# Edge sums moved to TensorE, and attended values computed one column at a time, in a four-layer stack

## The chip, the cores and the metric

The program runs on one core of a Trainium2 chip, in one launch. The core has TensorE (PE for matmuls, PEld for its weight loads), VectorE (DVE), ScalarE (ACT), GpSimd (POOL) and SyncE (SP), which here issues the DMAs. Everything is float32. SBUF and PSUM have 128 partitions[...]. The metric is device time in microseconds (us), the median over runs.

## What is computed

The input is four images of 56 x 56 positions with 128 channels. Four layers follow each other, each as `x = x + layer(group_norm(x))`. Two of them are touched by the change.

Layer 1, the edge layer, treats each of the 56 rows of an image as 56 nodes and sums over all ordered pairs of nodes in that row:

```python
proj_i = jnp.einsum('blnf,of->blno', x, W1)
proj_j = jnp.einsum('blnf,of->blno', x, W2)
edge = jax.nn.relu(proj_i[:, :, :, None, :] + proj_j[:, :, None, :, :] + be)
edge_sum = edge.sum(axis=3)
node_in = jnp.concatenate([x, edge_sum], axis=-1)
node = jax.nn.relu(jnp.einsum('blnc,oc->blno', node_in, Wn) + bn)
```

Written for one channel and one row, with a(n) from W1 and c(m) from W2 and the bias, the sum over m of relu(a(n) + c(m)) is wanted: 56 x 56 values for each row and channel.

Layer 2 is an attention of 32 heads over time steps, carried out on Fourier coefficients. Of it, only the attended values matter here:

```python
out = jnp.einsum('bhts,bhsd->bhtd', attn_w, vs)
...
projd = _fno_layer(out, wP, wPs, bPs, (H, W))
```

Since the projection adds up the heads, what is needed for each of 32 spectral columns c and 56 spectral rows r is the sum over heads h and steps s of attention(h, t, s) times a complex number d(h, c, r) times the complex spectrum x(s, c, r).

Layer 0 (window and global attention, MLP) and layer 3 (a convolution over rows and sums) are the same before and after.

## The kernel before

`build` runs layers 0 and 1 image by image (`first_layers`: window attention, global attention, MLP, then `edge_layer`, L539) and stores each image in `x2d`. Then it computes layer 2's spectra of all images (`spectra`), the weights d (`value_weights`), the attention weights (`attention_weights`), the attended values (`attend`, L916, and `attended_rows`, L973), and last, image by image, `operator_block` and `conv_layer`. Tiles come from pools; a pool's `bufs` is the number of copies that rotate, and a writer waits until the readers of the copy that it takes over are done. Except in the global attention of layer 0, whose TensorE order is written out by hand, the framework orders each engine's instructions, and adds the waits.

**Edge layer.** Channels lie on the partitions. A block (28 in all, 7 for each image) is 8 rows of 56 nodes, 448 columns. TensorE makes a (`e_pi`, L554) and c (`e_pj`, L558) in PSUM; ScalarE copies both into SBUF (`e_a`, L556; `e_c`, L560). For each of the 8 rows, a tile `e_e` of 56 x 56 = 3136 values per partition is filled with a(n) + c(m), on VectorE for even rows (L567, which reads c from PSUM) and on GpSimd for odd rows (L565, both operands from SBUF). ScalarE applies relu in place (L568), and VectorE sums over m (L569, `tensor_reduce` into `e_sum`). There are 4 copies of `e_e`. Two accumulated matmuls with Wn (L571, L572), relu with bias on ScalarE (`e_o`, L574) and an addition on VectorE (L575) end the block.

**Attended values.** `value_weights` writes d in three real combinations to DRAM (`dd`). `attend` runs over 4 groups of 8 columns, 3 combinations and 2 pairs of images. It loads d, spread over 56 partitions, into `u_d` (L932); ScalarE copies the spectrum into PSUM (`u_px`, L944). VectorE (L953, x from PSUM) multiplies into `u_ud`, GpSimd (L955, x from SBUF) into `u_up`, and TensorE (L958) sums over heads and steps with the attention `AT` as the stationary operand and 448 columns moving. `attended_rows` then transposes the result `y` on TensorE into `yh`, partitions by (re/im, r).

**Attention weights**, which the change leaves alone but which the prediction reads: for each head and for both q and k, VectorE multiplies (`q_a`, L863) and multiplies and adds (L867), GpSimd multiplies (`q_c`, L865) and adds (`q_q`, L869), VectorE adds a bias (L870), all on SBUF operands of 1792 (L870: 112) values per partition.

Of the kernel before, what the change touches and what calls it, by code (L numbers as in the profile page):

```python
# [39 lines left out]
def blk(j):  # L40
    return slice(j * NB, (j + 1) * NB)
# [496 lines left out]

def edge_layer(k, w, x1):  # L539

    nc, tc = k.nc, k.tc
    xf = x1.rearrange("p l n -> p (l n)")
    with ExitStack() as es:
# [6 lines left out]
        es_ = big.tile([P, HH, HH], F32, name="e_sum")  # L550
        esf = es_.rearrange("p l n -> p (l n)")
        for j in range(NBLK):
            pi = psum.tile([P, 512], F32, tag="pi", name="e_pi")
            nc.tensor.matmul(pi[:, :NB], w.W1, xg[:, blk(j)], start=True, stop=True)  # L554
            a = wk.tile([P, 8, HH], F32, name="e_a")
            nc.scalar.activation(a.rearrange("p l n -> p (l n)"), pi[:, :NB], AF.Identity, bias=w.be)  # L556
            pj = psum.tile([P, 512], F32, tag="pj", name="e_pj")
            nc.tensor.matmul(pj[:, :NB], w.W2, xg[:, blk(j)], start=True, stop=True)  # L558
            c = wk.tile([P, 8, HH], F32, name="e_c")
            nc.scalar.copy(c.rearrange("p l n -> p (l n)"), pj[:, :NB])  # L560
            pj3 = pj[:, :NB].rearrange("p (l n) -> p l n", l=8)
            for l in range(8):
                e = wk.tile([P, HH, HH], F32, name="e_e", bufs=4)
                if l % 2:
                    nc.gpsimd.tensor_add(e, bc(a[:, l, :], 2, HH), bc(c[:, l, :], 1, HH))  # L565
                else:
                    nc.vector.tensor_add(e, bc(a[:, l, :], 2, HH), bc(pj3[:, l, :], 1, HH))  # L567
                nc.scalar.activation(e, e, AF.Relu)  # L568
                nc.vector.tensor_reduce(es_[:, 8 * j + l, :], e, AX.X, ALU.add)  # L569
            po = psum.tile([P, 512], F32, tag="mm", name="e_po")  # L570
            nc.tensor.matmul(po[:, :NB], w.Wn[:, 0, :], xg[:, blk(j)], start=True, stop=False)  # L571
            nc.tensor.matmul(po[:, :NB], w.Wn[:, 1, :], esf[:, blk(j)], start=False, stop=True)  # L572
            o = wk.tile([P, NB], F32, name="e_o")
            nc.scalar.activation(o, po[:, :NB], AF.Relu, bias=w.bn)  # L574
            nc.vector.tensor_add(xf[:, blk(j)], xf[:, blk(j)], o)  # L575


def l1_host(i):
    We, Wn = i["L1_conv_We"], i["L1_conv_Wn"]
    return {  # L580
        "w1_W1": We[:, :P].T, "w1_W2": We[:, P:].T, "w1_be": i["L1_conv_be"].reshape(P, 1),
        "w1_Wn": Wn.T.reshape(2, P, P).transpose(1, 0, 2), "w1_bn": i["L1_conv_bn"].reshape(P, 1),
    }
# [176 lines left out]
def spectra(k, w, st, x2d):  # L760

    nc, tc = k.nc, k.tc
    with ExitStack() as es:
# [3 lines left out]
        for b in range(B):  # L767
# [23 lines left out]
            for c0 in range(0, 32, 4):  # L791
                ps = psum.tile([P, 512], F32, tag="acc", name="s_px")
                for i in range(4):
                    for ri in range(2):
                        nc.tensor.matmul(ps[:112, i * 112:(i + 1) * 112], z[:, ri, c0 + i, :], k.fv[:, 0, ri, :],
                                         start=(ri == 0), stop=(ri == 1))
                copy(k, c0 // 4, st.xh[:, b, :, c0:c0 + 4, :].rearrange("p i c r -> p c i r"),
                     ps[:112, :448].rearrange("p (c i r) -> p c i r", c=4, i=2))


def value_weights(k, I, w, dd):
# [3 lines left out]
    with ExitStack() as es:  # L805
# [18 lines left out]
        f = wk.tile([P, 3, 8, HH], F32, name="d_f")  # L824
# [4 lines left out]
        nc.scalar.copy(f[:, 0], d[:, 0])  # L829
        nc.vector.tensor_sub(f[:, 1], d[:, 1], d[:, 0])  # L830
        nc.vector.tensor_add(f[:, 2], d[:, 0], d[:, 1])
        nc.sync.dma_start(dd.rearrange("n g h i x -> (g h i) n x"), f.rearrange("p n c r -> p n (c r)"))


def attention_weights(k, I, w, st):

    nc, tc = k.nc, k.tc
    with ExitStack() as es:
# [63 lines left out]
        for bp in range(2):  # L902
# [4 lines left out]
            for h0 in range(0, 16, 4):  # L907
                pt = psum.tile([P, 4, P], F32, tag="mm", name="q_pt")
                for i in range(4):
# [3 lines left out]
                     pt[:112].rearrange("p h (b t) -> p h b t", b=2))  # L913


def attend(k, st, dd):  # L916

    nc, tc = k.nc, k.tc  # L920
    with ExitStack() as es:
        dk = es.enter_context(tc.tile_pool(name="u_dk", bufs=3))
        wk = es.enter_context(tc.tile_pool(name="u_wk", bufs=2))
        psum = es.enter_context(tc.tile_pool(name="u_ps", bufs=2, space=PSUM))
        for g in range(4):
            cs = slice(8 * g, 8 * g + 8)
            for n in (1, 2, 0):
                d = []
                for i in range(2):
                    t = dk.tile([112, 8, NB], F32, tag="d", name="u_d")  # L930
                    for h2 in range(2):
                        nc.sync.dma_start(t[56 * h2:56 * h2 + 56].rearrange("p h x -> p (h x)"),  # L932
                                          dd[n, g, h2, 8 * i:8 * i + 8].rearrange("h x -> (h x)").partition_broadcast(HH))
                    d.append(t)
                for bp in range(2):
                    bs = slice(2 * bp, 2 * bp + 2)
                    if n:
                        x = st.xh[:, bs, n - 1, cs, :].rearrange("p b c r -> p b (c r)")
                    else:
                        x = wk.tile([112, 2, NB], F32, name="u_x")  # L940
                        nc.gpsimd.tensor_add(x, *(st.xh[:, bs, i, cs, :].rearrange("p b c r -> p b (c r)")
                                                  for i in range(2)))
                    px = psum.tile([112, 2, 512], F32, name="u_px")
                    nc.scalar.copy(px[:, :, :NB], x)  # L944
                    po = psum.tile([P, 512], F32, tag="acc", name="u_po")
                    left = 16

                    for i in (0, 1) if bp == 0 else (1, 0):
                        for h0, m, e in ((0, 2, "d"), (5, 2, "p"), (2, 2, "d"), (4, 1, "d"), (7, 1, "p")):
# [235 lines left out]
```

## Time and profile before

| what | us |
|---|---|
| median of 3 runs (7187.75 to 7190.51) | 7190.48 |
| time of the profiled execution | 7190.51 |
| its span, from the first to the last instruction | 7188.7 |
| edge layer of the first image, `e_xg` to the last `e_o` (766.0 to 1072.0) | 306 |
| the same of the other three images (from 1813.9, 2861.8, 3913.1) | 306 each |
| `attention_weights` (4533.7 to 5294.9) | 761 |
| `attend`, first `u` to the last (5295.1 to 5645.2) | 350 |
| `attended_rows` (5645.3 to 5661.6) | 16 |

Times in views of the profile count from the first instruction. A row of the groups reads: line, engine, operation, output and inputs with shapes, number of instructions, then busy us in total, mean ns of one, and the idle time of the engine just before them with what ended it. A row of the timeline reads: start us, length us, engine, line, operation, tiles, how many instructions it merges, and in brackets the idle time before it and what ended that. One float32 matmul of the program shows as two MATMUL records, each with its own weight load. A duration counts from the moment that the engine takes up an instruction; a wait for a memory port lies within it.

### The profile page before, as it was taken

Reading aid. Unit: us, or ns where it says so; the run is one execution under the profiler, and the core shown is the slowest. Engines: PE = TensorE matmul, PEld = TensorE weight load, DVE = VectorE, ACT = ScalarE, POOL = GpSimd, SP = SyncE. Lnnn points to the kernel's source line nnn. Section 1 sums busy time; section 2 is a strip of 40 time slices with the busy share of each in tenths; the row PEclk is TensorE's granted clock in tenths of the full one; section 3 lists DMA queues with packets and bytes.
Section 4 is the critical chain, followed back from the end, with each engine's and each line's share of the span. In section 5 each row is a group of like instructions: output and inputs, shape, how many; then the busy total and the mean of one; then the engine's idle time right before and its main releaser. Section 6 shows DMA issues by size and latency. Waiting matters only on the chain.

```text
span 7188.7 us, 65062 instructions
## 1 busy us (share of the span) xinstructions
PE 4042.8 (56%) x28408; PEld 1841.6 (26%) x28408; DVE 4836.2 (67%) x2583; ACT 2497.7 (35%) x2060; POOL 2931.6 (41%) x791
## 2 busy tenths in 40 slices
PE   5888316898226897127896125422258754535363
PEld 3222103222013222013222014322223433323142
DVE  4797794895985995985995973688867533333333
ACT  2564452664543663544663532000000111111111
POOL 2453442552533552533552520577769311111111
PEclk6998656998556998557997556555579755555556
DMA  0000000000000000000000010000035100000000
GB/s 18 1 1 1 9 9 1 1 1 1 9 9 1 1 1 9 0 9 1 1 1 0 0 50 10 7 1 1 1 72 117 36 1 18 1 18 1 18 1 9
DMA packets 14102, 79.93 MB, mean 11 GB/s; under 512 B 5642, under 2 KB 7866, under 8 KB 8434
## 3 DMA queue, kind: packets, MB, share of 16 engines
q1 hardware_dynamic: 13810, 75.69, 3.8%
q8 instruction: 225, 3.69, 0.2%
q14 instruction: 67, 0.55, 0.0%
HBM read 62.15 MB, written 13.53 MB: 11 GB/s over the span
## 4 chain that ended last, share of the span: by engine, by line
DVE 51%; PE 32%; POOL 8%; ACT 5%; issue 3%; DMA 1%; SPq 0%; POOLq 0%; DVEq 0%; ACTq 0%
DVE f_accd L396 16%; DVE e_sum L569 10%; DVE e_e L567 5%; DVE q_q L870 3%; POOL q_q L869 3%; PE u_po L958 2%; PE f_s L438 2%; DVE q_a L863 2%; PE id_pw L735 2%; PE f_po L402 2%; PE id_pv L730 2%; DVE q_a L867 2%; PE sc_ps L750 2%; PE w_pt L242 1%; PE o_pk L1017 1%
## 5 line engine op out<-in xcount | busy, mean ns | idle before, releaser
L396 DVE TENSOR_TENSOR f_accd<-f_accd,f_ring 128x1792 f32<-128x1792 f32 x392 | 1410.0, 3597 | 90.9 <-ACT f_ring L440 54.1
L440 ACT ACTIVATE f_ring<-f_s 128x1792 f32<-128x1792 f32 (+3 forms) x796 | 1119.1, 1431 | 529.0 <-PE f_s L438 360.9
L396 POOL TENSOR_TENSOR f_accp<-f_accp,f_ring 128x1792 f32<-128x1792 f32 x168 | 833.9, 4964 | 412.1 <-ACT f_ring L440 410.2
L438 PE MATMUL f_s<-f_qT,f_kT 32*128 32x448 f32 x5376 | 835.5, 604 | 132.6 <-ACT f_ring L440 129.1
L565 POOL TENSOR_TENSOR e_e<-e_a,e_c 128x3136 f32<-128x3136 f32 x112 | 610.1, 5449 | 576.5 <-DVE e_sum L569 521.8
L569 DVE TENSOR_REDUCE e_sum<-e_e 128x56 f32<-128x3136 f32 x224 | 749.6, 3404 | 6.8 <-ACT e_e L568 6.8
L568 ACT ACTIVATE e_e<-e_e 128x3136 f32<-128x3136 f32 x224 | 621.0, 2810 | 279.7 <-POOL e_e L565 183.3
L402 PE MATMUL f_po<-f_ring,f_va 128*32 128x448 f32 x5376 | 658.7, 569 | 0.0
L438 PEld LDWEIGHTS f_s<-f_qT,f_kT 32*128 32x128 f32 x5376 | 257.8, 188 | 714.4 <-ACT f_ring L440 380.5
L567 DVE TENSOR_TENSOR e_e<-e_a,e_pj 128x3136 f32<-128x3136 f32 x112 | 379.1, 3407 | 16.0 <-ACT e_c L560 16.0
L396 POOL TENSOR_TENSOR f_accp<-f_ring 128x1792 f32<-128x1792 f32 x28 | 121.2, 4329 | 608.1 <-ACT f_ring L440 608.1
L869 POOL TENSOR_TENSOR q_q<-q_a,q_c 128x1792 f32<-128x1792 f32 x64 | 308.0, 4813 | 143.8 <-DVE q_a L867 143.8
L558 PE MATMUL e_pj<-e_xg,t_w_W 128*128 128x448 f32 x56 | 47.7, 952 | 490.9 <-DVE e_e L567 490.9
L572 PE MATMUL e_po<-e_sum,t_w_Wn 128*128 128x448 f32 x56 | 52.1, 1033 | 471.0 <-DVE e_sum L569 471.0
L953 DVE TENSOR_TENSOR u_ud<-u_px,u_d 112x1792 f32<-112x1792 f32 x144 | 239.3, 1707 | 99.7 <-PE u_po L958 89.3
L875 PE MATMUL q_pp<-q_q,c_sym 128*128 128x112 f32 x64 | 23.7, 474 | 500.1 <-DVE q_q L870 500.1
L870 DVE TENSOR_SCALAR q_q<-q_q,q_bias 128x112 f32<-128x112 f32 x64 | 202.4, 3162 | 130.8 <-POOL q_q L869 130.8
L865 POOL TENSOR_TENSOR q_c<-iS,t_w_qk 128x1792 f32<-128x1792 f32 x64 | 253.9, 3969 | 7.2 <-DMA t_w_qk<-in_w_qk 2.4
L876 ACT COPY q_q<-q_pp 128x112 f32<-128x112 f32 x32 | 8.1, 252 | 709.1 <-PE q_pp L875 709.1
L701 POOL TENSOR_TENSOR o_m<-o_m,in_r 128x3136 f32<-128x3136 f32 x12 | 65.3, 5445 | 424.5 <-DVE in_r L700 424.5
L232 POOL TENSOR_TENSOR w_sm<-w_sm,w_max 98x1568 f32<-98x1568 f32 x32 | 89.8, 2807 | 359.3 <-DVE w_max L231 269.8
L402 PEld LDWEIGHTS f_po<-f_ring,f_va 128*32 128x32 f32 x5376 | 112.5, 110 | 464.8 <-issue 456.0
(316 smaller groups left out, 7406.1 us busy)
## 6 DMA issues: line engine op xcount, KB each, us to landing
u_d<-dd SPq DMA_DIRECT2D x48, 784.0 KB
xw<-in_x SPq DMA_DIRECT2D x4, 1568.0 KB
x2d<-x SPq DMA_DIRECT2D x4, 1568.0 KB
s_x<-x2d SPq DMA_DIRECT2D x4, 1568.0 KB
o_x<-x2d SPq DMA_DIRECT2D x4, 1568.0 KB
out<-v_y SPq DMA_DIRECT2D x4, 1568.0 KB
t_w_qk<-in_w_qk SPq DMA_DIRECT2D x1, 1024.0 KB
dd<-d_f SPq DMA_DIRECT2D x1, 672.0 KB
```

Of the source, the lines that this page charges most:

```text
L396: e.tensor_add(acc[a], before, slots(j, c))
L402: nc.tensor.matmul(po[heads[h], :NB], va[o, c, heads[h]], p, start=(c == 0), stop=(c == 24))
L438: nc.tensor.matmul(ss[:, i, :NB], kT[heads[h], c * P:(c + 1) * P], qT[heads[h], blk(j)], start=True, stop=True)
L440: nc.scalar.activation(ring[:, slot:slot + m, :], ss[:, :m, :NB], AF.Exp, scale=scale)
L565: nc.gpsimd.tensor_add(e, bc(a[:, l, :], 2, HH), bc(c[:, l, :], 1, HH))
L567: nc.vector.tensor_add(e, bc(a[:, l, :], 2, HH), bc(pj3[:, l, :], 1, HH))
L568: nc.scalar.activation(e, e, AF.Relu)
L569: nc.vector.tensor_reduce(es_[:, 8 * j + l, :], e, AX.X, ALU.add)
L865: nc.gpsimd.tensor_mul(c, st.iS, bc(bc(w.qk[:, x, 1, h, :], 1, 2), 3, HH))
L869: nc.gpsimd.tensor_add(q, a, c)
L870: nc.vector.tensor_scalar_add(q[:, :, 0, :], q[:, :, 0, :], bias[:, x, h:h + 1])
L953: nc.vector.tensor_mul(u, bc(px[:, :, :NB], 2, m), dm)
```

## The change

The edge layer and the attended values are both rewritten.

In the edge layer, c is stored negated, -(c + be), so that max(a, -c) = relu(a + c) - c. A step now covers 4 values of m for all 8 rows and 56 nodes: 1792 values per partition. The 14 steps of a block follow the string "ddpddpdpddpddp": for the 9 "d" steps, VectorE takes the maximum alone, a from PSUM and c from SBUF; for the 5 "p" steps, GpSimd subtracts and ScalarE applies relu. The sum over m is made by TensorE: for each step 16 matmuls with blocks of 32 x 32 of the identity, which add channel quarter r of slice q into partition quarter q of PSUM bank r of `e_acc`. ScalarE copies the four banks (`e_sums`), and Wn's second half is applied to each bank by a matmul of its own, with weights repeated for the four partition quarters (`Wnq`). What the maximum leaves out, -c summed over the 36 values of m that VectorE takes, is `e_rest`, fed to one more matmul.

The attended values go column by column: for each of 32 columns the two parts of d are loaded (`u_d`, two copies), and for each image VectorE multiplies by the real part, GpSimd by the imaginary part, VectorE subtracts one half and GpSimd adds the other; 16 matmuls, one for each pair of heads, have the product stationary and 56 columns of attention moving. Their result is already in the layout of `yh`, so `attended_rows` is gone. `value_weights` writes d in 16 DMAs instead of three combinations in one.

```diff
+EDGE_TURNS = "ddpddpdpddpddp"
...
+    nd = 4 * EDGE_TURNS.count("d")
+    quarters = [slice(32 * q, 32 * q + 32) for q in range(4)]
...
-        es_ = big.tile([P, HH, HH], F32, name="e_sum")
-        esf = es_.rearrange("p l n -> p (l n)")
         for j in range(NBLK):
-            pi = psum.tile([P, 512], F32, tag="pi", name="e_pi")
-            nc.tensor.matmul(pi[:, :NB], w.W1, xg[:, blk(j)], start=True, stop=True)
-            a = wk.tile([P, 8, HH], F32, name="e_a")
-            nc.scalar.activation(a.rearrange("p l n -> p (l n)"), pi[:, :NB], AF.Identity, bias=w.be)
-            pj = psum.tile([P, 512], F32, tag="pj", name="e_pj")
-            nc.tensor.matmul(pj[:, :NB], w.W2, xg[:, blk(j)], start=True, stop=True)
+            pa = psum.tile([P, 512], F32, tag="pa", name="e_pa")
+            nc.tensor.matmul(pa[:, :NB], w.W1, xg[:, blk(j)], start=True, stop=True)
+            a = wk.tile([P, NB], F32, name="e_a")
+            nc.scalar.copy(a, pa[:, :NB])
+            pc = psum.tile([P, 512], F32, tag="mm", name="e_pc")
+            nc.tensor.matmul(pc[:, :NB], w.W2, xg[:, blk(j)], start=True, stop=True)
             c = wk.tile([P, 8, HH], F32, name="e_c")
-            nc.scalar.copy(c.rearrange("p l n -> p (l n)"), pj[:, :NB])
-            pj3 = pj[:, :NB].rearrange("p (l n) -> p l n", l=8)
-            for l in range(8):
-                e = wk.tile([P, HH, HH], F32, name="e_e", bufs=4)
-                if l % 2:
-                    nc.gpsimd.tensor_add(e, bc(a[:, l, :], 2, HH), bc(c[:, l, :], 1, HH))
+            nc.vector.tensor_scalar(c.rearrange("p l m -> p (l m)"), pc[:, :NB], w.be, -1.0, ALU.add, ALU.mult)
+            rest = wk.tile([P, 8], F32, name="e_rest")
+            nc.vector.tensor_reduce(rest, c[:, :, 0:nd], AX.X, ALU.add)
+            nc.vector.tensor_scalar_mul(rest, rest, -1.0)
+            acc = psum.tile([P, 4, 512], F32, name="e_acc", bufs=1)
+            at = {"d": 0, "p": nd}
+            for g, e in enumerate(EDGE_TURNS):
+                t = wk.tile([P, 4, 8, HH], F32, tag="e_" + e, name="e_t" + e, bufs=4 if e == "d" else 3)
+                cm = bc(c[:, :, at[e]:at[e] + 4].rearrange("p l m -> p m l"), 3, HH)
+                at[e] += 4
+                if e == "d":
+                    am = bc(pa[:, :NB].rearrange("p (l n) -> p l n", l=8), 1, 4)
+                    nc.vector.tensor_tensor(t, am, cm, ALU.max)
                 else:
-                    nc.vector.tensor_add(e, bc(a[:, l, :], 2, HH), bc(pj3[:, l, :], 1, HH))
-                nc.scalar.activation(e, e, AF.Relu)
-                nc.vector.tensor_reduce(es_[:, 8 * j + l, :], e, AX.X, ALU.add)
+                    nc.gpsimd.tensor_sub(t, bc(a.rearrange("p (l n) -> p l n", l=8), 1, 4), cm)
+                    tf = t.rearrange("p m l n -> p (m l n)")
+                    nc.scalar.activation(tf, tf, AF.Relu)
+                for q in range(4):
+                    for r, o in enumerate(quarters):
+                        nc.tensor.matmul(acc[quarters[q], r, :NB], k.ident[o, o],
+                                         t[o, q].rearrange("p l n -> p (l n)"),
+                                         start=(g == 0), stop=(g == len(EDGE_TURNS) - 1))
+            sums = wk.tile([P, 4, NB], F32, name="e_sums")
+            nc.scalar.copy(sums, acc[:, :, :NB])
             po = psum.tile([P, 512], F32, tag="mm", name="e_po")
             nc.tensor.matmul(po[:, :NB], w.Wn[:, 0, :], xg[:, blk(j)], start=True, stop=False)
-            nc.tensor.matmul(po[:, :NB], w.Wn[:, 1, :], esf[:, blk(j)], start=False, stop=True)
+            nc.tensor.matmul(po[:, :NB].rearrange("p (l n) -> p l n", l=8), w.Wn[:, 1, :], bc(rest, 2, HH),
+                             start=False, stop=False)
+            for r in range(4):
+                nc.tensor.matmul(po[:, :NB], w.Wnq[:, r, :], sums[:, r, :], start=False, stop=(r == 3))
             o = wk.tile([P, NB], F32, name="e_o")
             nc.scalar.activation(o, po[:, :NB], AF.Relu, bias=w.bn)
...
+    W2 = Wn[:, P:].T.reshape(4, 1, 32, P)
...
+        "w1_Wnq": np.broadcast_to(W2, (4, 4, 32, P)).reshape(4, P, P).transpose(1, 0, 2),
...
-                copy(k, c0 // 4, st.xh[:, b, :, c0:c0 + 4, :].rearrange("p i c r -> p c i r"),
-                     ps[:112, :448].rearrange("p (c i r) -> p c i r", c=4, i=2))
+                copy(k, c0 // 4, st.xh[:, c0:c0 + 4, b, :], ps[:112, :448].rearrange("p (c r) -> p c r", c=4))
...
-        f = wk.tile([P, 3, 8, HH], F32, name="d_f")
...
-        nc.scalar.copy(f[:, 0], d[:, 0])
-        nc.vector.tensor_sub(f[:, 1], d[:, 1], d[:, 0])
-        nc.vector.tensor_add(f[:, 2], d[:, 0], d[:, 1])
-        nc.sync.dma_start(dd.rearrange("n g h i x -> (g h i) n x"), f.rearrange("p n c r -> p n (c r)"))
+        for cq in range(4):
+            for h2 in range(2):
+                p0 = 32 * cq + 16 * h2
+                for ri in range(2):
+                    nc.sync.dma_start(dd[h2, 8 * cq:8 * cq + 8, :, ri, :].rearrange("c h r -> h c r"), d[p0:p0 + 16, ri])
...
-                     pt[:112].rearrange("p h (b t) -> p h b t", b=2))
+                     pt[:112].rearrange("p h (b t) -> p h b t", b=2)[:, :, :, :HH])
...
-        dk = es.enter_context(tc.tile_pool(name="u_dk", bufs=3))
...
-        for g in range(4):
-            cs = slice(8 * g, 8 * g + 8)
-            for n in (1, 2, 0):
...
-                    nc.scalar.copy(px[:, :, :NB], x)
...
-                    for i in (0, 1) if bp == 0 else (1, 0):
-                        for h0, m, e in ((0, 2, "d"), (5, 2, "p"), (2, 2, "d"), (4, 1, "d"), (7, 1, "p")):
-                            u = wk.tile([112, 2, 2, NB], F32, tag="u_" + e, name="u_u" + e)[:, :, :m, :]
-                            dm = bc(d[i][:, h0:h0 + m, :], 1, 2)
-                            if e == "d":
-                                nc.vector.tensor_mul(u, bc(px[:, :, :NB], 2, m), dm)
-                            else:
-                                nc.gpsimd.tensor_mul(u, bc(x, 2, m), dm)
-                            for q in range(m):
-                                for b2 in range(2):
-                                    nc.tensor.matmul(po[64 * b2:64 * b2 + 64, :NB],
-                                                     st.AT[:, 8 * i + h0 + q, 2 * bp + b2, :], u[:, b2, q, :],
...
-def attended_rows(k, st):
...
+        for c in range(32):
+            d = wk.tile([112, 16, 2, HH], F32, name="u_d")
+            for h2 in range(2):
+                nc.sync.dma_start(d[56 * h2:56 * h2 + 56].rearrange("p h i r -> p (h i r)"),
+                                  dd[h2, c].rearrange("h i r -> (h i r)").partition_broadcast(HH))
+            po = psum.tile([P, 512], F32, tag="acc", name="u_po")
+            for b in range(B):
+                x = bc(st.xh[:, c, b, :].rearrange("p (i r) -> p i r", i=2), 1, 16)
+                u = wk.tile([112, 16, 2, HH], F32, name="u_u")
+                v = wk.tile([112, 16, 2, HH], F32, name="u_v")
+                nc.vector.tensor_mul(u, x, bc(d[:, :, 0, :], 2, 2))
+                nc.gpsimd.tensor_mul(v, x, bc(d[:, :, 1, :], 2, 2))
+                nc.vector.tensor_sub(u[:, :, 0, :], u[:, :, 0, :], v[:, :, 1, :])
+                nc.gpsimd.tensor_add(u[:, :, 1, :], u[:, :, 1, :], v[:, :, 0, :])
+                for hp in range(16):
+                    nc.tensor.matmul(po[:112, b * HH:(b + 1) * HH], u[:, hp].rearrange("p i r -> p (i r)"),
+                                     st.AT[:, hp, b, :], start=(hp == 0), stop=(hp == 15))
+            nc.scalar.copy(st.yh[:, :, c], po[:112, :B * HH])
...
-            st.xh = xp.tile([112, B, 2, 32, HH], F32, name="xh")
-            st.AT = xp.tile([112, 16, B, 64], F32, name="AT")
+            st.xh = xp.tile([112, 32, B, 112], F32, name="xh")
+            st.AT = xp.tile([112, 16, B, HH], F32, name="AT")
...
-            ys = ExitStack()
-            rp = ys.enter_context(tc.tile_pool(name="y", bufs=1, side="right"))
-            st.y = rp.tile([P, 2, 32, 2, HH], F32, name="y")
+            yp = es.enter_context(tc.tile_pool(name="yh", bufs=1, side="right"))
+            st.yh = yp.tile([112, B * HH, 32], F32, name="yh")
             attend(k, st, dd)
-        yp = es.enter_context(tc.tile_pool(name="yh", bufs=1))
-        st.yh = yp.tile([112, B * HH, 32], F32, name="yh")
-        attended_rows(k, st)
-        ys.close()
```

## Prediction

> **What bounds the kernel now.** I read the page first (busy time, chain), then one table of windows for the stages concerned, then the timeline inside each. The chain says which work ends last:
>
> ```profile
> DVE f_accd L396 16%; DVE e_sum L569 10%; DVE e_e L567 5%; DVE q_q L870 3%; POOL q_q L869 3%; PE u_po L958 2%; PE f_s L438 2%; DVE q_a L863 2%; PE id_pw L735 2%; PE f_po L402 2%; PE id_pv L730 2%; DVE q_a L867 2%; PE sc_ps L750 2%; PE w_pt L242 1%; PE o_pk L1017 1%
> ...
> 5295.00:5645.00 350.00, 303.67 (x1536) 112.56 (x1536) 247.02 (x160) 30.93 (x41) 306.57 (x104) 0.97 0.49 111
> 4540.00:5290.00 750.00, 209.09 (x4252) 196.21 (x4251) 598.97 (x269) 13.12 (x35) 567.46 (x130) 0.57 0.00 1
> 766.00:1072.00 306.00, 46.46 (x56) 14.21 (x56) 297.70 (x91) 166.12 (x77) 152.52 (x28) 0.51 0.00 0
> ```
>
> The window rows give stretch and length, busy time (instructions) of PE, PEld, DVE, ACT and POOL, granted TensorE clock, DMA share, GB/s. The edge layer (766 to 1072) is VectorE alone: 297.70 of 306 us. The attended values (5295 to 5645) use PE and POOL at 87% each at almost full clock. The attention weights (4540 to 5290) look odd: DVE and POOL together are busy 1166 us in 750, yet the work is a fixed pattern of short operations. The timelines explain:
>
> ```profile
> 800.31 13.39 DVE L569 TENSOR_REDUCE e_sum<-e_e 128x56 f32<-128x3136 f32 x4
> 813.62 3.41 DVE L567 TENSOR_TENSOR e_e<-e_a,e_pj 128x3136 f32<-128x3136 f32 x1
> 816.94 2.77 DVE L575 TENSOR_TENSOR x<-x,e_o 128x448 f32<-128x448 f32 x1
> ...
> 4805.02 3.95 POOL L869 TENSOR_TENSOR q_q<-q_a,q_c 128x1792 f32<-128x1792 f32 x1 [2.21 <-DVE q_a L867]
> 4805.60 5.26 DVE L863 TENSOR_TENSOR q_a<-S,t_w_qk 128x1792 f32<-128x1792 f32 x1
> 4809.05 4.85 POOL L865 TENSOR_TENSOR q_c<-iS,t_w_qk 128x1792 f32<-128x1792 f32 x1
> 4810.78 3.20 DVE L870 TENSOR_SCALAR q_q<-q_q,q_bias 128x112 f32<-128x112 f32 x1
> 4813.90 2.07 DVE L867 SCALAR_TENSOR_TENSOR q_a<-R,t_w_qks,q_a 128x1792 f32<-128x1792 f32 x1
> ...
> 5404.31 6.05 POOL L955 TENSOR_TENSOR u_up<-xh,u_d 112x1792 f32<-112x1792 f32 x2 [0.72 <-PE u_po L958]
> 5405.76 4.95 DVE L953 TENSOR_TENSOR u_ud<-u_px,u_d 112x1792 f32<-112x1792 f32 x3 [1.96 <-PE u_po L958]
> ```
>
> Look at ends. POOL L869 ends at 4808.97; DVE L863, taken up at 4805.60, ends 1.89 us after that, though it needs 2.01 us when alone. POOL L865, taken up at 4809.05, ends 3.12 us after that DVE ends (3.19 alone). One runs, then the other. In the last two rows both run together at full speed: there VectorE's x lies in PSUM. The same at 816.94: 2.77 us for 448 values with both operands in SBUF, 0.62 without GpSimd.
>
> **What the Trainium skill says.** "GPSIMD Engine Reference", section 1: GpSimd's SBUF interfaces are shared with VectorE, with contention for VectorE instructions in a 2-port mode or with two SBUF inputs. The trace agrees and shows the size: full exclusion. "VectorE: DVE Perf Modes", "Why PSUM operands drop a tier": an operand in PSUM keeps an operation out of the 2-port mode; the trace agrees (L567 beside L565: 3407 ns at most 3422). "TensorE: Matmul & The Clock Gate", Part 3: 16 tiles of 32 x 32 together were measured at 10.6 times one after the other. No run here shows 16; four together are seen below. Its Part 1 says that the clock knows two states, half and full, by activity: agrees with 0.51 in the idle edge stage and 0.97 above.
>
> **The change, part 1: attended values.** Removed: 350 us (with 10.4 us for the first DMA, by the idle time before L953) and 16.4 us of `attended_rows`. Added: 32 x 4 = 128 turns of two multiplications of 1792, one subtraction and one addition of 896, now all with two SBUF operands. So VectorE and GpSimd exclude each other and the four add up. VectorE 1792: 2.01 (L863). GpSimd 1792 with neither operand repeated along the innermost axis: 4.00 (L955). VectorE 896: 1.08 (L953). GpSimd 896: 2.09 (L941). Sum 9.18 us. In the attention weights such a sum, 2.01 + 2.07 + 3.19 + 3.95 = 11.22, took 11.1 us a turn (22.19 us for two, 4799.57 to 4821.76), since part of the start-up hides under the other's turn. I take 9.0 us. Bounds: 8.6 (0.12 to 0.15 of start-up hidden at each of the four, as L863's 1.89 against 2.01 shows) and 9.5 (each handover a further 0.08). The instructions go in pairs of images; a new product needs TensorE to have read the one two turns back. TensorE has 32 records a turn, each with a new weight load of 112 columns: at half clock L1017 takes 213 ns a record (128 columns), so 187 ns and 6.0 us a turn, beside the 9 us. ScalarE's copy of 224 values hides too, and the loads, 784 KB for every 36 us, are a fifth of today's 111 GB/s. First load 10 us as now; 7 us at the end, the last 16 matmuls and the copy. 128 x 9.0 + 17 = 1169 us. Against 366.5: **+803 us** (+755 to +866). The 16 small DMAs of `value_weights` stand in SP's queue ahead of the last image's load, which waits for its buffer anyway; spectra and attention weights keep their work: nothing, at most 5 us.
>
> **Part 2: edge layer.** Removed: 1224 us (4 x 306). Added for each block:
> - VectorE: 9 maxima of 1792, a in PSUM, so no exclusion: 2.01 each (L953), 1.96 back to back, 17.6 us; c 0.68 (L179); a reduction of 288 values 0.44 (3.40 for 3136, start-up 0.14); two SBUF-only operations, `e_rest` 0.1 and x 0.63, which can be held up by GpSimd: up to 3.2 each, with GpSimd 70% busy I take 0.7 together beyond what the block's end costs anyway.
> - GpSimd: 5 subtractions with one repeated operand, 3.19 (L865), 16.0 us, beside VectorE. ScalarE: 5 relus of 1792 (1.6 from L568's 2.81 for 3136), copies 0.53 and 1.6, relu 0.63: 10.8 us.
> - TensorE: 14 x 16 matmuls. Now four tiles stream together:
>
> ```profile
> 300.31 0.96 PE L402 MATMUL f_po<-f_ring,f_va 128*32 128x448 f32 x8
> 301.20 1.03 PE L438 MATMUL f_s<-f_qT,f_kT 32*128 32x448 f32 x8
> 302.17 0.96 PE L402 MATMUL f_po<-f_ring,f_va 128*32 128x448 f32 x8
> ```
>
> Eight records, four tiles with two each, take 0.93 us (1.86 for two lines, 300.31 to 302.17), by columns as by rows. If 16 go together as four do, a step costs 0.95 us at full clock, 13.3 us a block. Ten matmuls of full height take 0.75 each at full clock (the pair of L571 records took 1.50 at half clock, 771.08 to 772.58): 7.5 us. Together 20.8, just below the block time that follows; four of the ten can fill TensorE's wait for the sums' copy.
>
> The block's end decides. In the order of the changed kernel, ScalarE's copy of a for the next block stands, for most blocks, behind the copy of the sums, and the next block's maxima and subtractions wait for it. After VectorE's last maximum: the last "d" step 0.95, the last "p" step 0.95, copy of the sums 1.6, copy of a 0.53: 4.0 us, in which c and the reduction (1.1) go beside. So a block is 17.6 + 0.1 + 0.63 + 4.0 + 0.7 = **23 us** where 42.6 were. GpSimd's loop is nearly as long: 16.0 + 1.0 held up + relu 1.6 + 0.95 + 1.6 + 0.53 = 21.7. An image: 4.5 to the first copy of a (769.84 + 0.63, as now), 6 x 23, and 27 for the last block to its end: 169.5. 4 x (306 - 169.5) = **-546 us** (T = 21: -594; T = 29.5, TensorE often at half clock: -380).
>
> **Sum.** 7188.7 + 803 - 546 = 7446. The profiled execution is 1.8 us longer than its span and equals the median, so 7447 us.
>
> **Rivals.**
> - TensorE becomes the edge layer's bound: only eight tiles together, or half clock throughout, 1.86 us a step. A block is 14 x 1.86 + 7.5 = 33.5; an image 4.5 + 6 x 33.5 + 37 = 242.5; saving 254; 7188.7 + 803 - 254 = 7738. For it: 0.51 today, and no 16 tiles in the trace. Against: the stage would keep TensorE busy, and at 87% busy the clock is 0.97. 0.12.
> - The other side, faster: VectorE and GpSimd overlap in the new attended values. Without exclusion GpSimd's 4.00 + 2.09 is the longest of a turn; with 6.3 us: 128 x 6.3 + 17 - 366.5 = +457; with -546, 7100. It decides from a turn below 7.1 us, where 128 turns lose no more than the edge layer gains. For it: different operations and 112 partitions. Against: all 64 turns of the attention weights take turns. 0.06.
> - The attended values bound by TensorE: load and stream of one record not overlapped at half clock, 280 ns, and a late pair: 10 us a turn, +128, 7575. L1017 speaks against it. 0.05.
>
> **How the numbers follow.** Forecast 0.77, the three rivals 0.12, 0.06, 0.05. The forecast's own ends are 7188.7 + 755 - 594 = 7350 and 7188.7 + 866 - 380 = 7675; I cut the upper to 7650, which takes in the last rival. What a measurement can tell from no change is 0.2%, 14 us; a cancellation to that is left 0.01. Faster 0.06, same 0.01, slower 0.93.
>
> **What would show it.** Right: the edge stage at some 170 us an image with VectorE about 85% busy and waiting once a block for ScalarE; attended values of some 1170 us, in which DVE and POOL rows overlap in the list but end one after the other, and durations above 2.01 and 4.00. A PE share near 100% in the edge stage would show the first rival, a turn of 6 us the second, waits of VectorE for PE in the attended values the third. Wrong altogether if the edge stage gains more than 800 us, or hardly at all.

## The result and the profile after

The changed kernel takes 7492.52 us (median of 4 runs, 7486.17 to 7498.56), the kernel before 7190.49 (4 runs, 7187.75 to 7196.61): a ratio of 1.042 (1.040 to 1.044, 95% interval). The forecast was 7447, with a range of 7350 to 7650. The profiled execution took 7498.56, its span is 7496.5.

| stage, profiled execution | before, us | after, us | difference | forecast |
|---|---|---|---|---|
| edge layer, four images | 4 x 306 | 186.2, 186.2, 186.9, 186.1 | -479 | -546 |
| attended values, from the end of the attention weights to the last `yh` | 367 | 1126 | +759 | +803 |
| spectra | 295 | 310 | +15 | 0 to 5 |
| global attention of layer 0, four images | 2047 | 2056 | +9 | 0 |
| all else | | | +4 | 0 |
| span | 7188.7 | 7496.5 | +308 | +257 |

The page's chain of waits of the changed kernel, by engine and by line ("issue" is time in which an engine waited for nothing that the profile shows):

```profile
PE 43%; DVE 35%; issue 8%; POOL 7%; ACT 5%; DMA 1%; SPq 0%; POOLq 0%; DVEq 0%; ACTq 0%
DVE f_accd L396 14%; PE u_po L962 10%; PE f_s L438 3%; DVE e_td L579 3%; DVE q_q L895 3%; PE f_po L402 3%; POOL q_q L894 3%; DVE q_a L888 2%; PE id_pw L761 2%; PE id_pv L756 2%; DVE q_a L892 2%; PE e_acc L586 2%; PE sc_ps L776 2%; ACT f_ring L440 2%; PE w_pt L242 1%
```

`e_sum` and `e_e`, 15% before, are gone; in the edge layer `e_td` and `e_acc` with 5% stand for them. The attended values, 2% before, are 10%, and the chain puts them down to TensorE's `u_po`. The windows of the two stages (stretch, length, busy us and instructions of PE, PEld, DVE, ACT and POOL, granted clock, DMA share, GB/s):

```profile
767.00:954.00 187.00, 149.24 (x3248) 66.42 (x3248) 148.00 (x93) 78.47 (x57) 114.90 (x35) 0.96 0.01 2
4839.00:5964.00 1125.00, 778.57 (x4096) 769.36 (x4096) 644.57 (x256) 16.87 (x32) 983.37 (x256) 0.50 0.10 23
```

The edge layer runs at nearly full clock now, and no engine is busy over 80%. The attended values run at half clock, with GpSimd at 87% and TensorE at 69%. One edge block in the timeline of the changed kernel:

```profile
843.45 1.02 PE L592 MATMUL e_po<-e_xg,t_w_Wn 128*128 128x448 f32 x2
844.30 0.92 PE L593 MATMUL e_po<-e_rest,t_w_Wn 128*128 128x448 f32 x2
845.05 0.92 PE L565 MATMUL e_pc<-e_xg,t_w_W 128*128 128x448 f32 x2
...
846.08 0.68 DVE L567 TENSOR_SCALAR e_c<-e_pc,t_w_be 128x448 f32<-128x448 f32 x1 [4.75 <-PE e_pc L565]
846.80 0.45 DVE L569 TENSOR_REDUCE e_rest<-e_c 128x8 f32<-128x288 f32 x1
846.91 16.50 POOL L581 TENSOR_TENSOR e_tp<-e_a,e_c 128x1792 f32<-128x1792 f32 x5 [9.55 <-DVE e_c L567]
847.17 2.01 DVE L579 TENSOR_TENSOR e_td<-e_pa,e_c 128x1792 f32<-128x1792 f32 x1
...
849.10 1.09 DVE L570 TENSOR_SCALAR e_rest<-e_rest 128x8 f32<-128x8 f32 x1
850.10 2.01 DVE L579 TENSOR_TENSOR e_td<-e_pa,e_c 128x1792 f32<-128x1792 f32 x1
...
852.45 1.41 DVE L599 TENSOR_TENSOR x<-x,e_o 128x448 f32<-128x448 f32 x1 [0.33 <-ACT e_o L598]
...
853.78 13.60 DVE L579 TENSOR_TENSOR e_td<-e_pa,e_c 128x1792 f32<-128x1792 f32 x7
...
872.13 0.68 DVE L567 TENSOR_SCALAR e_c<-e_pc,t_w_be 128x448 f32<-128x448 f32 x1 [4.75 <-PE e_pc L565]
```

From one `e_c` to the next, 26.05 us. Follow VectorE: nine maxima take 17.5 us, c and its reduction 1.1, `e_rest` 1.0 (eight columns; it ends as the first GpSimd L581 does, which started at 846.91), x 1.3 after a wait of 0.3, and 4.75 us go to a wait for the matmul `e_pc`. That matmul stands in TensorE's order behind the last two steps and two matmuls of the block's end (843.45, 844.30). Two turns of the attended values, in the same kernel's timeline:

```profile
5398.54 10.53 POOL L958 TENSOR_TENSOR u_v<-xh,u_d 112x1792 f32<-112x1792 f32 x2
5403.07 2.17 DVE L957 TENSOR_TENSOR u_u<-xh,u_d 112x1792 f32<-112x1792 f32 x1 [3.55 <-PE u_po L962]
...
5409.03 2.07 POOL L960 TENSOR_TENSOR u_u<-u_u,u_v 112x896 f32<-112x896 f32 x1
5409.04 3.94 DVE L957 TENSOR_TENSOR u_u<-xh,u_d 112x1792 f32<-112x1792 f32 x1 [3.80 <-PE u_po L962]
5412.91 3.97 DVE L959 TENSOR_TENSOR u_u<-u_u,u_v 112x896 f32<-112x896 f32 x2
...
5414.13 12.16 PE L962 MATMUL u_po<-AT,u_u 112*112 112x56 f32 x64 [5.18 <-DVE u_u L959]
5415.89 10.53 POOL L958 TENSOR_TENSOR u_v<-xh,u_d 112x1792 f32<-112x1792 f32 x2
```

A pair of turns takes 17.35 us (5398.54 to 5415.89). Two explanations fit it equally well. The first is that VectorE and GpSimd exclude each other: 2 x (2.01 + 4.00 + 1.08 + 2.09) less what each start hides. The second is a loop through TensorE: 64 records that take 12.2 us together free `u_u`, then come the multiply, the subtraction and TensorE again. The brackets and the chain name only the second. They had to be told apart by experiment.

### The profile page after: what moved, and what is told of

It reads as the page before. It is cut to its first block, busy times and chain, and to the rows that moved or that the text cites. A ratio compares the mean times of both kernels' runs of the same rounds, so it can differ in the third digit from the quotient of the medians.

```text
span 7496.5 us, 96515 instructions
## 1 busy us (share of the span) xinstructions
PE 4945.2 (66%) x43672; PEld 2725.8 (36%) x43672; DVE 4638.0 (62%) x2669; ACT 2126.2 (28%) x1959; POOL 3448.4 (46%) x971
## 4 chain that ended last, share of the span: by engine, by line
PE 43%; DVE 35%; issue 8%; POOL 7%; ACT 5%; DMA 1%; SPq 0%; POOLq 0%; DVEq 0%; ACTq 0%
DVE f_accd L396 14%; PE u_po L962 10%; PE f_s L438 3%; DVE e_td L579 3%; DVE q_q L895 3%; PE f_po L402 3%; POOL q_q L894 3%; DVE q_a L888 2%; PE id_pw L761 2%; PE id_pv L756 2%; DVE q_a L892 2%; PE e_acc L586 2%; PE sc_ps L776 2%; ACT f_ring L440 2%; PE w_pt L242 1%
## 5 line engine op out<-in xcount | busy, mean ns | idle before, releaser
L962 PE MATMUL u_po<-AT,u_u 112*112 112x56 f32 x4096 | 778.6, 393 | 346.9 <-DVE u_u L959 326.5
L962 PEld LDWEIGHTS u_po<-AT,u_u 112*112 112x112 f32 x4096 | 769.4, 306 | 356.2 <-issue 335.6
L957 DVE TENSOR_TENSOR u_u<-xh,u_d 112x1792 f32<-112x1792 f32 x128 | 389.9, 3047 | 471.5 <-PE u_po L962 457.2
L958 POOL TENSOR_TENSOR u_v<-xh,u_d 112x1792 f32<-112x1792 f32 x128 | 673.6, 5282 | 16.8 <-DMA u_d<-dd 16.8
L581 POOL TENSOR_TENSOR e_tp<-e_a,e_c 128x1792 f32<-128x1792 f32 x140 | 459.7, 3312 | 273.2 <-DVE e_c L567 232.5
L579 DVE TENSOR_TENSOR e_td<-e_pa,e_c 128x1792 f32<-128x1792 f32 x252 | 492.8, 2008 | 0.0
L586 PE MATMUL e_acc<-e_td,c_ident 32*32 32x448 f32 x8064 | 301.3, 560 | 126.4 <-DVE e_td L579 126.4
L960 POOL TENSOR_TENSOR u_u<-u_u,u_v 112x896 f32<-112x896 f32 x128 | 314.6, 2459 | 125.6 <-DVE u_u L957 125.6
L964 ACT COPY yh<-u_po 112x224 f32<-112x224 f32 x32 | 17.3, 539 | 1108.2 <-PE u_po L962 1058.7
L583 ACT ACTIVATE e_tp<-e_tp 128x1792 f32<-128x1792 f32 x140 | 237.7, 1698 | 288.0 <-POOL e_tp L581 288.0
```

Of the source, the lines that this page charges most:

```text
L579: nc.vector.tensor_tensor(t, am, cm, ALU.max)
L581: nc.gpsimd.tensor_sub(t, bc(a.rearrange("p (l n) -> p l n", l=8), 1, 4), cm)
L586: nc.tensor.matmul(acc[quarters[q], r, :NB], k.ident[o, o], t[o, q].rearrange("p l n -> p (l n)"), start=(g == 0), stop=(g == len(EDGE_TUR ...
L957: nc.vector.tensor_mul(u, x, bc(d[:, :, 0, :], 2, 2))
L958: nc.gpsimd.tensor_mul(v, x, bc(d[:, :, 1, :], 2, 2))
L962: nc.tensor.matmul(po[:112, b * HH:(b + 1) * HH], u[:, hp].rearrange("p i r -> p (i r)"), st.AT[:, hp, b, :], start=(hp == 0), stop=(hp == ...
```

## The experiments

Line numbers are those of each kernel and shift by some lines. The kernel before was measured anew beside each group of runs, and its median moved a little (7190 to 7203 us); so ratios to it, with 95% intervals, are compared, beside stage times of the profiled execution. From here on, the stage of the attended values counts from its first multiplication to the last `yh`, 1120 us in the changed kernel (the 1126 above begin some 6 us earlier, at the end of the attention weights).

**Do the parts add up?** One run has the new edge layer with the attended values of before, one the reverse.

> The edge layer of the change alone, with the attended values of the kernel before (weights stationary over three products, no change of the spectra). My theory: the two parts of the change stand in different stages and add up, so this run shows the edge layer's stage at 186 us an image instead of 306, as in the changed kernel, and the attended values at 350 us as before: 7190 - 4 x 119.8 = 6711 us, between 6690 and 6740. Rival: the granted clock is shared between the stages, and the edge layer's busier TensorE takes it from the stages that follow (the spectra of the changed kernel were 15 us slower at half clock in their first image): then the stages outside the edge layer grow by some 15 us each and the run comes to 6730 to 6790. Rival on the other side: the edge layer does not carry the gain at all, 7190.

> The attended values of the change alone (with its order of x and of the weights, and its DMAs), with the edge layer of the kernel before. My theory, parts that add up: 7190 + 753 (attended values 1119.6 in place of 350 + 16.4) + 15 (spectra) = 7958 us, between 7930 and 7990. Rival, if the 15 us of the spectra come from the clock that the new edge layer leaves behind rather than from the 16 weight DMAs of an image: the spectra are back at 295 us and the run is at 7943 or a little less. If instead the spectra stay at 310 us here, the DMAs and the half clock in them belong to the attended values' part.

Edge layer alone: 6718.77 us, ratio 0.933 (0.930 to 0.936), 186.2 us an image. Attended values alone (two runs): 7969.01, ratio 1.107 (1.103 to 1.111), 1121 us for the stage against 1120 in the changed kernel. The parts add up: -0.067 + 0.107 = +0.040 where the whole has +0.042. The edge layer alone is a better kernel than the one before.

The spectra took 296 us in the first run and 289 in the second: neither part makes them 310. The window of the spectra in the changed kernel, and in the run `e6_early` below, which has the spectra, weights and single DMA of the kernel before:

```profile
3769.00:4078.00 309.00, 199.94 (x1178) 153.08 (x1179) 122.03 (x162) 59.57 (x86) 21.79 (x4) 0.61 0.06 21
```

```profile
3792.00:4103.00 311.00, 200.07 (x1179) 153.40 (x1180) 123.65 (x165) 60.16 (x87) 21.79 (x4) 0.61 0.06 22
```

The same length and the same clock, 0.61, with the old code; runs of 289 to 296 us show 0.65 to 0.67, again with old and new code. So these 15 us go with the clock granted at that moment, not with the 16 DMAs; why the clock differs from run to run is not shown. The 9 us of the global attention move in the same way from run to run (511 to 517 us an image in the edge layer alone).

**What sets a turn of the attended values?** Three edits to the changed kernel: more buffers, x from PSUM, and both.

```diff
-                u = wk.tile([112, 16, 2, HH], F32, name="u_u")
-                v = wk.tile([112, 16, 2, HH], F32, name="u_v")
+                u = wk.tile([112, 16, 2, HH], F32, name="u_u", bufs=4)
+                v = wk.tile([112, 16, 2, HH], F32, name="u_v", bufs=4)
```

```diff
-                nc.vector.tensor_mul(u, x, bc(d[:, :, 0, :], 2, 2))
+                px = psum.tile([112, 512], F32, name="u_px")
+                nc.scalar.copy(px[:, :112], st.xh[:, c, b, :])
+                nc.vector.tensor_mul(u, bc(px[:, :112].rearrange("p (i r) -> p i r", i=2), 1, 16), bc(d[:, :, 0, :], 2, 2))
```

> The changed kernel with four buffers in place of two for u and v of the attended values. A turn is 8.7 us now. Theory of my prediction (the four elementwise operations of a turn exclude each other, 2.0 + 1.0 + 3.9 + 1.9 = 8.7 us of a path that only one of VectorE and GpSimd can use): more buffers change nothing, 7490, between 7470 and 7500. Rival (the loop TensorE, u buffer, VectorE multiply, lock wait, subtraction, TensorE is what turns, since each pair of multiplies waits for TensorE's release of u): with buffers to run ahead the turn falls to what the slowest engine needs, GpSimd 5.9 us or TensorE 6.0 us: 128 x 2.7 = 345 us less at most, 7145 to 7290.

> The changed kernel with x copied into PSUM by ScalarE (a new 112x112 copy a turn), so that VectorE's multiply has one input from PSUM and one from SBUF; still two buffers for u and v. Exclusion theory: the multiply, 2.0 us a turn, no longer stands on the shared path, and the path holds 1.0 + 3.9 + 1.9 = 6.8 us a turn: 128 x 1.9 = 240 us less, 7250, between 7200 and 7330. Rival (TensorE and the two buffers of u set the turn): the lock wait before the multiply of 2 us in a pair of turns goes, 64 x 2 = 130 us less, 7360, between 7330 and 7400. If VectorE's multiply waits for GpSimd in spite of the input from PSUM: 7490.

> Both edits together: four buffers for u and v, and x read from PSUM by VectorE's multiply. Exclusion theory: the same as with x in PSUM alone, 6.8 us a turn: 7250, between 7200 and 7300. Rival (TensorE and buffers): 6.0 us a turn, TensorE's 32 records of 187 ns at half clock: 128 x 2.7 = 345 us less, 7145, between 7110 and 7200.

| edit | median, us | ratio | stage, us | a pair of turns |
|---|---|---|---|---|
| none (changed kernel) | 7492.52 | 1.042 (1.040 to 1.044) | 1120 | 17.35 |
| four buffers | 7511.44 | 1.043 (1.039 to 1.048) | 1116 | 17.2 |
| x in PSUM | 7366.79 | 1.026 (1.023 to 1.028) | 1003 | 15.5 |
| both | 7268.02 | 1.013 (1.009 to 1.016) | 892 | 13.66 |

Four buffers alone gain nothing, though they take away the wait that the chain named. The timeline of that run, where neither VectorE nor GpSimd waits for TensorE any more:

```profile
5398.39 7.76 DVE L959 TENSOR_TENSOR u_u<-u_u,u_v 112x896 f32<-112x896 f32 x2
5400.37 9.62 POOL L958 TENSOR_TENSOR u_v<-xh,u_d 112x1792 f32<-112x1792 f32 x2
5406.08 9.61 DVE L957 TENSOR_TENSOR u_u<-xh,u_d 112x1792 f32<-112x1792 f32 x2
...
5409.96 7.68 POOL L960 TENSOR_TENSOR u_u<-u_u,u_v 112x896 f32<-112x896 f32 x2
...
5415.61 7.75 DVE L959 TENSOR_TENSOR u_u<-u_u,u_v 112x896 f32<-112x896 f32 x2
```

Both engines have no gap, and rows overlap all the time; yet a VectorE multiply takes 4.8 us on average where it needs 2.0 alone, and a subtraction 3.9 where it needs 1.1. Two engines that shared a path at half speed each would also look stretched like this. The ends of the single instructions, which the rows above merge, speak against it: put in order of their ends, each comes after the one before, of whichever engine, by its own time alone less a start of 0.12 to 0.16 us. A VectorE multiply ends 1.89 us after it (2.01 alone), a subtraction 0.95 (1.08), a GpSimd multiply 3.84 (4.00), an addition 1.94 (2.09). So while one works the other waits, inside its own instruction. That is exclusion, and it alone holds the turn at 8.6 us. With x in PSUM the multiply leaves the shared path, and two rows of the run with both edits show it:

```profile
5424.91 9.61 POOL L960 TENSOR_TENSOR u_v<-xh,u_d 112x1792 f32<-112x1792 f32 x2
5430.60 2.01 DVE L959 TENSOR_TENSOR u_u<-u_px,u_d 112x1792 f32<-112x1792 f32 x1
```

VectorE's 2.01 us lie wholly within GpSimd's 9.61. What is left on the path, 1.08 + 4.00 + 2.09 = 7.2 less the hidden starts, is the 6.83 us a turn that this run shows. With two buffers it does not get there: the run with x in PSUM alone stops at 7.8 us, near where the rival had put it (7360 us). So the loop through TensorE is a second limit, 0.9 us behind the first. It hides half of what taking the multiply off the path brings (117 us with two buffers, 224 with four), and the first limit hides nearly all of what more buffers bring (4 us alone, 111 on top of x in PSUM).

**What sets an edge block?** All of the following have the attended values of before and are measured against the edge layer alone. The first moves the next block's projections (a, c, reduction and rest) ahead of the step numbered 7 (of 0 to 13). The second has the rest scaled on ScalarE as well, and the third has the latter alone. The fourth has the rest on ScalarE and the projections between the last step and the block's end.

```diff
-        for j in range(NBLK):
+        def project(j):
...
+            return pa, a, c, rest
+
+        ahead = project(0)
+        for j in range(NBLK):
+            pa, a, c, rest = ahead
...
+                if g == 7 and j + 1 < NBLK:
+                    ahead = project(j + 1)
```

```diff
-            nc.vector.tensor_scalar_mul(rest, rest, -1.0)
+            nc.scalar.mul(rest, rest, -1.0)
```

> The edge layer alone as in the run before, with one move: the two projections of the next block (matmuls, copy, c, its reduction and the scaling of the rest) are issued before step 7 of 14 of the present block, not after its end. Theory (VectorE sets the block and 4.75 us of it are a wait for the late projection matmul): the block falls from 26.05 to about 21.5 us, 28 blocks x 4.5 = 126 us less than the edge layer alone, 6585, between 6560 and 6620. Rival: GpSimd's five steps and their ReLU, or TensorE with 14 steps x 1.1 us + block end = 17.5 us, take the wait's place and the block stays above 24 us: 6650 to 6711.

> As the run with the early projection, with the scaling of the rest (128x8, 1.09 us on VectorE with the wait for a GpSimd instruction that holds the path both use) on ScalarE. Theory: VectorE loses 1.0 us a block and is the bound, 28 x 1.0 = 28 us less, 6557, between 6530 and 6590. Rival: the wait for GpSimd moves to the next instruction with two inputs from SBUF (the addition to x) or ScalarE's pass comes late for the mean's matmul, and nothing is gained: within 8 us of the run before.

> The edge layer alone, in the order of the changed kernel, with the scaling of the rest (128x8) on ScalarE. Theory: the 1.0 us that this 8-column instruction holds VectorE, nearly all of it a wait for a GpSimd instruction, is on the path of the block: 28 x 1.0 = 28 us less than the edge layer alone, 6690, between 6670 and 6705. Rival: the wait moves on to the next two-input instruction (the addition to x, which now waits 0.8 us), or the block is set by TensorE: no gain, 6710 to 6730.

> The edge layer alone (attended values of the kernel before), the rest scaled on ScalarE, and the projections of the next block issued after the last step of a block and ahead of its block end, instead of before step 7. In the run with the move before step 7 the block was 27.5 us in place of 26.05: the copy of the single accumulator (4 banks of PSUM) stood behind two ReLUs of the next block on ScalarE, and TensorE began the next block 12.9 us after the last step. Theory: with the projections there, VectorE has c early and ScalarE's copy of the sums stands ahead of those ReLUs; the block falls to 22 to 24 us, 28 x 3 = 84 us less than the edge layer alone, 6635, between 6600 and 6690. Rival: the single accumulator sets the block (14 steps, copy, and TensorE's eight records of the block end before the next block's first step), and the block stays within 1 us of 26: 6690 to 6750.

None gains, and my theory fell in all four. In the run with the early projections VectorE no longer waits for `e_pc`, but a block takes 27.5 us. Its timeline at a block's end:

```profile
844.52 1.44 PE L592 MATMUL e_acc<-e_tp,c_ident 32*32 32x448 f32 x27
...
846.43 1.70 ACT L589 ACTIVATE e_tp<-e_tp 128x1792 f32<-128x1792 f32 x1 [3.68 <-POOL e_tp L587]
...
849.65 1.70 ACT L589 ACTIVATE e_tp<-e_tp 128x1792 f32<-128x1792 f32 x1 [1.51 <-POOL e_tp L587]
...
851.25 1.63 ACT L596 COPY e_sums<-e_acc 128x1792 f32<-128x1792 f32 x1
...
858.78 2.05 PE L592 MATMUL e_acc<-e_td,c_ident 32*32 32x448 f32 x59
```

The sums are complete at 845.96, but ScalarE copies them at 851.25: with c early, GpSimd starts early, and its first two products of the next block have their relu ahead of the copy in ScalarE's order, which the framework made (in the program's text the copy comes first). `e_acc` (a tile of 4 x 512 values for each partition) exists once; TensorE can't begin the next block before the copy, and by then its clock has dropped (the eight `Wnq` records take 5.92 us instead of 3.17). The rest on ScalarE alone changes nothing either: the hold of 1.0 us goes, and the wait of x for `e_o` grows from 0.33 to 1.34. With the projections after the last step the copy does come in time (845.49, ahead of the relus), but c is late again: VectorE waits 3.55 us for `e_pc` and 2.65 for `e_o`. Hence one more edit on top of the second: a relu of a "p" step takes its bias, zero times a sum, from a tile that ScalarE writes after the copy of the sums.

```diff
-                    nc.scalar.activation(tf, tf, AF.Relu)
+                    nc.scalar.activation(tf, tf, AF.Relu, bias=zero)
...
             nc.scalar.copy(sums, acc[:, :, :NB])
+            zero = wk.tile([P, 1], F32, name="e_zero")
+            nc.scalar.mul(zero, sums[:, 0, 0:1], 0.0)
```

> The run with the early projection and the rest on ScalarE, and one more edit: each ReLU of the p steps takes its bias, zero times a sum, from a 128x1 tile that ScalarE writes after it has copied the previous block's sums, so that the copy of the single accumulator can no longer stand behind the next block's ReLUs on ScalarE. Theory (the early projection gained nothing since that copy came 6 us late, 851.25 in place of about 846, and TensorE could not begin the next block): the block falls from 26.8 in the run without this edit to 22 to 23.5 us, 28 blocks x 3.5 = 100 us less than the edge layer alone: 6620, between 6590 and 6670. Rival: something else holds the block (the addition to x that waits for TensorE's block end, or GpSimd's five steps): within 1 us of 26, 6690 to 6740.

| run (attended values of before in all) | median, us | ratio | first image, us | a block |
|---|---|---|---|---|
| edge layer alone | 6718.77 | 0.933 (0.930 to 0.936) | 186.2 | 26.05 |
| projections before step 7 | 6765.61 | 0.938 (0.935 to 0.942) | 191.6 | 27.5 |
| the same, rest on ScalarE | 6739.52 | 0.936 (0.934 to 0.939) | 188.3 | 27.2 |
| rest on ScalarE alone | 6730.82 | 0.934 (0.930 to 0.938) | 186.2 | 26.05 |
| projections after the last step, rest on ScalarE | 6726.15 | 0.937 (0.933 to 0.940) | 187.8 | 26.6 |
| before step 7, rest on ScalarE, sums first | 6595.79 | 0.916 (0.914 to 0.917) | 156.7 | 20.6 |

The timeline of the last one:

```profile
848.65 0.67 DVE L566 TENSOR_SCALAR e_c<-e_pc,t_w_be 128x448 f32<-128x448 f32 x1
849.35 0.45 DVE L568 TENSOR_REDUCE e_rest<-e_c 128x8 f32<-128x288 f32 x1
...
849.72 7.81 DVE L585 TENSOR_TENSOR e_td<-e_pa,e_c 128x1792 f32<-128x1792 f32 x4
...
851.53 1.65 ACT L596 COPY e_sums<-e_acc 128x1792 f32<-128x1792 f32 x1 [1.47 <-PE e_acc L592]
...
853.50 1.79 ACT L589 ACTIVATE e_tp<-e_tp,e_zero 128x1792 f32<-128x1792 f32 x1
...
858.77 0.89 DVE L607 TENSOR_TENSOR x<-x,e_o 128x448 f32<-128x448 f32 x1 [1.24 <-ACT e_o L606]
...
859.58 9.73 DVE L585 TENSOR_TENSOR e_td<-e_pa,e_c 128x1792 f32<-128x1792 f32 x5
...
869.24 0.67 DVE L566 TENSOR_SCALAR e_c<-e_pc,t_w_be 128x448 f32<-128x448 f32 x1
```

ScalarE now waits for TensorE, not the reverse, the relu comes after, and VectorE has one wait of 1.24 us in a block of 20.6. The block fell further than expected (22 to 23.5 us). TensorE sets it now, as the window of this block shows (same order of numbers as above):

```profile
848.65:869.24 20.59, 20.59 (x493) 11.48 (x479) 19.32 (x13) 11.97 (x10) 16.17 (x5) 1.00 0.01 3
```

Its records leave no gap in 20.59 us, at full clock; they are the 14 steps and ten matmuls that the prediction had put at 20.8 us. In the changed kernel the same records fill 20.6 of 26.05 us. This is the fastest kernel found, 8.4% below the one before (8.3 to 8.6%). The gain needed both early projections and an early copy: the runs with one of the two stay at 26.05 to 27.5 us a block. Whether it needs the rest on ScalarE too was not tried. The edge layer's loss against my forecast is thereby placed: it was the order around the block's end, not the work.

## Why the prediction was right, and where its terms were off

- **Attended values, +803, measured +759.** The step that carried the result is that the four operations add up, since VectorE and GpSimd exclude each other. The runs with four buffers and with x in PSUM show it. A turn was taken at 9.0 us and is 8.67, within the bounds of 8.6 and 9.5: the starts hide 0.13 us at each of the four operations. That is 42 of the 44 us.
- **"TensorE ... 6.0 us a turn, beside the 9 us".** The size was right (64 records in 12.2 us), but the cover was thinner than the sentence says: with two buffers TensorE's time is part of a loop of 7.8 us a turn. It cost nothing here only because 8.6 is more.
- **Edge layer, -546, measured -479.** The mis-sized terms are those of the block, 23 us, measured 26.05 once the layer runs evenly. "After VectorE's last maximum ... 4.0 us": 4.75. C and the reduction were to "go beside" this wait; they come after it, 1.1 us. `e_rest`, x and the holds, 0.1 + 0.63 + 0.7: 2.7 with the wait for `e_o`. Together 3.05 us. The first two of an image's six periods were shorter (21.6 and 25.7 us from first maximum to first maximum), so the six took 151.6 us where 6 x 23 = 138 were taken. The start took 6.5 (taken 4.5) and the last block 28.1 (taken 27). That is 16.7 us an image, 67 in four. I had also named the wrong wait: VectorE waits for TensorE and not for ScalarE. It is c that comes late, through `e_pc` in TensorE's order, and a's copy (871.30 to 871.83 in the block after the one shown) is done before it. VectorE is busy 79%, not 85%.
- **A step of TensorE, 0.95 us.** Right: in the second block of the first image its 14 steps follow each other without a gap, from 804.65 to 818.19, 13.5 us where 13.3 were forecast. All 16 tiles go together, and the first rival, TensorE as the edge layer's bound at half clock, is out for this change: 149 of 187 us busy at a clock of 0.96. At full clock TensorE is the bound once the order is mended, as the last run shows.
- **The rival on the other side** (VectorE and GpSimd overlap) is refuted for operands in SBUF and is what happens with x in PSUM, which was not the change. Even so, and with four buffers, a turn of 6.83 us leaves the kernel 1.3% slower than before (0.9 to 1.6%). I had put the change of sides at a turn "below 7.1 us"; by my own terms it is 7.0, and with the measured 479 us of the edge layer 6.5.
- **The attended values bound by TensorE at 10 us a turn**: no; its records take 187 ns as forecast.
- **Spectra and weights "nothing, at most 5 us"**: +15 in this execution, with the clock, as shown; with the global attention and small rest it adds to what the two main errors leave over: -44 + 67 + 28 = 51, from 257 to 308 (28 is 15 + 9 and 4 elsewhere). That the total came within 51 us is in part luck, since the errors of the two stages have opposite signs.
- **Slips that move nothing.** POOL L865 ends 3.04 us after DVE L863 by the lines shown, not 3.12 (that is counted from the start of the next row). A turn of 8.6 us gives +751, not +755. L567 shows only that VectorE isn't held up by GpSimd when one operand lies in PSUM; in which mode it ran no trace here shows.

## What to carry to other kernels

When both VectorE and GpSimd get elementwise work with two SBUF operands, add their durations instead of taking the longer, and put one of VectorE's operands into PSUM before anything else is tuned. A chain of waits names one of several limits that may lie close together (8.6 and 7.8 us a turn here, and it named the wrong one): before removing the one it names, work out the period of the next. Where work for the next round is moved forward, look at what it lets other engines put in front of the present round's last step, on every in-order queue it touches.

## What the runs showed of the hardware

- **Waiting counts as busy.** In the run with four buffers VectorE and GpSimd are busy 1098 and 1100 of 1115 us. Idle time does not show the exclusion; only durations against those of the same shape alone do (4.8 against 2.0 us).
- **Half clock at 89% busy.** The window of the attended values in the run with both edits:

```profile
4846.00:5700.00 854.00, 760.72 (x3995) 749.96 (x3995) 653.32 (x247) 42.24 (x152) 844.38 (x248) 0.50 0.11 28
```

  TensorE has records for 89% of the time and the clock stays at 0.50; in the attended values of the kernel before, records for 87% of the time went with 0.97. What differs is the kind: a new weight load of 112 columns for every 56 columns that stream, as against 448 streaming. The Trainium skill, "TensorE: Matmul & The Clock Gate", Part 1, lets the clock follow how busy the array has been; busy time as the profile counts it does not tell that. Whether weight loads don't count was not tried.
- **16 tiles together in float32.** In the edge layer of the changed kernel, the 448 records of 14 steps take 13.5 us (804.65 to 818.19), 0.97 a step. At 0.375 us for one full-height record (0.75 from the pair at 844.30 to the next) one after the other they would take 168 us by estimate, 12.4 times as long; the same page, Part 3, measured 10.6 times for 16 tiles.
